# Cycle steps first: a new order of work in seven slots of a two-layer kernel's first attention phase

## Chip, cores and metric

The kernel runs on one core of a Trainium2 chip. The metric is the device time of one execution in microseconds (us). Engines are named as in the profile: PE (TensorE matmul), PEld (its weight loads), DVE (VectorE), ACT (ScalarE), POOL (GpSimd), SP (SyncE, here a DMA queue).

## The reference, cut to what matters

Two layers work on x of 32 sequences, 128 positions, 128 channels, in fp32. Each layer adds an attention block and a feed-forward block to x. Only the first layer is touched by the change:

```
h   = modulated(x, cond_1024)                 # per-sequence scaling around a 128x128 weight
x   = x + causal_attention(h, 16 heads of 64, length 256) @ W_out
f,i = sigmoid(x @ W_f.T + b_f), sigmoid(x @ W_i.T + b_i);  c = x @ W_h.T + b_h
F   = gated recurrence over the positions with f/(f+i+eps) and i/(f+i+eps)*c, starting from cond_1024
g   = sigmoid of a three-layer gelu net on the mean of F over positions
for cycle in 0, 1, 2:
    t = sigmoid of a four-layer gelu net on F (widths 128, 64, 32, 1)
    F = F + (0.1 + range*(0.7*g + 0.3*t - 0.5)*2) * twist(F)      # twist: channel quarters exchanged, with signs
x   = x + F
```

The second layer begins with a mixture of four experts of which two are chosen per sequence from means of x (`routed` computes the choice), then attention with 16 heads of 8, a low-rank modulated layer, and a slot-attention block. Its code is unchanged but for the moment at which the choice of experts and some constants are computed.

## The kernel before

x is held transposed in SBUF as 8 column groups of 128 x 512 (`col(g)`, 4 sequences of 128 positions each).

**The first phase** is a loop over h = 0..15 (a group g = h//2 and one half of the heads) and b = 0..3 (a sequence). One pass of the inner loop is called a *slot* here and numbered 4h+b, so 0 to 63. `unit(h, b)` returns the stages of one attention unit:

- `scores`: 16 matmuls and 2 mask matmuls into two PSUM banks; per bank a DVE maximum (tile `s_max`, 128x384 in), a minimum and an addition (`s_sb<-ps,s_max`); then on ACT four 128x128 exponentials and one 128x256; then POOL folds the rows (`s_half`, two `s_part`), DVE sums and inverts (`s_sum`), and POOL multiplies (`s_sb<-s_sb,s_sum`).
- `turned`: six transposes on PE; the four large ones are copied to `pT` by ACT (128x512), the two small ones by DVE (128x256).
- `values`: 16 small matmuls, copied to `oT` by DVE.
- `projected`: only for b = 3; four matmuls, added to `col(g)` by DVE.

`Staggered(0, 3, 4, 5)` runs, in each slot, the scores of the newest unit, `turned` of the unit three slots older, `values` of the one four older and `projected` of the one five older, in this order. Each slot also issues three of the twelve 128x512 projection matmuls (*pieces*) of h+1; their results go through ACT (`qk`, `v`), and for v an SP transfer (`vo`).

Woven between are generators, one step per slot: `recurrence(g)` starts at b = 1 of each odd h from 3 on (3 matmuls, ACT sigmoids, then on DVE two reciprocals of 128x256, eight scans and one scan of 128x512, with POOL products between). `twisted(g0, cyc, turned)` is one cycle for two groups; it runs at b = 2 of h = 6, 7, 8 (groups 0 and 1, cyc 0, 1, 2: slots 26, 30, 34), of h = 10, 11, 12 (slots 42, 46, 50) and of h = 14 (slot 58, cyc 0). Later cycles run in the second phase. It has four stages: `first` (cn_w1, two gelus of 128x512), `second` (cn_w2), `third` (cn_w3), `fourth` (cn_w4, two tanhs, then the coupling: on DVE `th` from a scalar_tensor_tensor; with cyc 0 a twist matmul whose bank is TF, otherwise TF is the tile `tw`; v = th x F on POOL; th x TF on DVE; F + th; tw = TF - v). In a slot with a cycle the stages alternate with the pieces: first, piece, second, piece, third, piece, fourth, all after the attention stages of that slot. In slot 58 `prepared()` (constants of the second layer) is issued before `first`. `routed` starts at b = 3 of h = 8 and 12 (slots 35 and 51), one step per slot.

**Order.** A scheduler may reorder PE, DVE and POOL instructions; ACT calls made through `act` keep program order, and instructions issued while `pinned` is set keep theirs (DVE and PE). The exponential and the gelu need different ACT tables, and a change between them shows as ACT_TABLE_LOAD.

**PSUM** has 8 banks, given out in turn by `ps()` (ring `AABBBCCC`), so a matmul into a bank waits for the reader of the bank's earlier content.

Nearly all calls go through helpers, so the profile gives line 259 for PE, DVE and POOL and line 383 for ACT; tiles, not lines, tell the operations apart.

Of the kernel before, what the change touches and what calls it, by code (L numbers as in the profile page):

```python
# [11 lines left out]
F32 = mybir.dt.float32  # L12
# [3 lines left out]
AF = mybir.ActivationFunctionType  # L16
ALU = mybir.AluOpType
AX = mybir.AxisListType

P = 128  # L20
# [5 lines left out]
CH = CB * S  # L26
# [192 lines left out]
class Staggered:  # L219
# [7 lines left out]
        self.items.append(stages)  # L227
        self._step()

    def _step(self):  # L230
        for k, lag in enumerate(self.lags):
            n = self.t - lag
            if 0 <= n < len(self.items) and k < len(self.items[n]) and self.items[n][k]:
                self.items[n][k]()
        self.t += 1

    def flush(self):
# [7 lines left out]
def program(ctx, tc, out, xT, packs, where):  # L245
    nc = tc.nc
    pinned = []
# [17 lines left out]
    V, T, G, A = Pinned(nc.vector, pinned), Pinned(nc.tensor, pinned), Pinned(nc.gpsimd, pinned_g), nc.scalar  # L265
# [17 lines left out]
    def w(name):  # L283
        pack, rows, c0, n = where[name]
        return loaded[pack][:rows, c0 : c0 + n]
# [6 lines left out]
    short = []  # L292

    def bank(tag):
        return psum.tile([P, 512], F32, tag="ps" + tag, name="ps", bufs=RING.count(tag))

    def ps():
        if short:
            return bank("C")
        turn["all"] += 1  # L300
        return bank(RING[(turn["all"] - 1) % 8])
# [5 lines left out]
    def mm(out_, lhsT, rhs, start=True, stop=True):  # L307
        T.matmul(out_, lhsT=lhsT, rhs=rhs, start=start, stop=stop)
# [9 lines left out]
    def tt(eng, out_, a, b, op):  # L318
        eng.tensor_tensor(out_, a, b, op)
# [10 lines left out]
    def b3(ap):  # L330

        return ap.rearrange("p (b s) -> p b s", s=S)
# [48 lines left out]
    def act(*args, **kwargs):  # L381

        return tc.keep_in_program_order(A.activation(*args, **kwargs))  # L383
# [7 lines left out]
    tpool = ctx.enter_context(tc.tile_pool(name="t2", bufs=2, side="right"))  # L391
# [29 lines left out]
    ar3 = const("ar3", w("arange"), 0.3)  # L421

    hTs, qks, vs, oTs = {}, {}, {}, {}

    def modulated(g):
        bs = slice(g * CB, (g + 1) * CB)
# [34 lines left out]
    def unit(h, b):  # L461
# [4 lines left out]
        g = h // 2  # L466
        cs = bass.ts(b, S)
        q2 = slice(b * S, b * S + 64), slice(b * S + 64, b * S + S)
        at = {}
# [49 lines left out]
        def turned():  # L519
            pT = apool.tile([P, 6, S], F32, tag="pT", name="pT", bufs=3)  # L520
            p = ps()
            for i in range(4):
                T.transpose(p[:, bass.ts(i, S)], at["s"][:, i, :], ident)
            act(pT[:, 0:4], b3(p), AF.Copy)
            p = ps()
            for i in range(2):
                T.transpose(p[:, bass.ts(i, S)], at["s"][:, 4 + i, :], ident)
            V.tensor_copy(pT[:, 4:6], b3(p)[:, 0:2])
            at["pT"] = pT
# [24 lines left out]
    Fs = {}  # L554
# [39 lines left out]
    def twisted(g0, cyc, turned):  # L594

        gs = (g0, g0 + 1)
        bs = slice(g0 * CB, (g0 + 2) * CB)
        nb = 2 * CB
        at = {}

        def first():
            at["h1"] = []
            for g in gs:
                p = ps()
                mm(p, w("cn_w1"), Fs[g])
                h1 = mpool.tile([P, CH], F32, tag="h1", name="h1")
                act(h1, p, AF.Gelu, bias=w("cn_b1"))
                at["h1"].append(h1)
            if cyc == 0:
                gct = mpool.tile([P, nb], F32, tag="gct", name="gct")  # L610
                for k, g in enumerate(gs):
                    V.tensor_reduce(gct[:, k * CB : (k + 1) * CB], b3(Fs[g]), AX.X, ALU.add)
                V.tensor_scalar(gct, gct, 1.0 / S, None, ALU.mult)
                p = ps()
                mm(p[:64, :nb], w("gc_w1"), gct)
                at["g1"] = mpool.tile([64, nb], F32, tag="g1", name="g1")
                act(at["g1"], p[:64, :nb], AF.Gelu, bias=w("gc_b1"))

        def second():

            p = ps()
            for k in range(2):
                mm(p[64 * k : 64 * k + 64], w("cn_w2"), at["h1"][k])
            at["h2"] = mpool.tile([P, CH], F32, tag="h2", name="h2", bufs=1)
            act(at["h2"], p, AF.Gelu, bias=w("cn_b2"))
            if cyc == 0:
                p = ps()
                mm(p[:32, :nb], w("gc_w2"), at["g1"])
                at["g2"] = mpool.tile([32, nb], F32, tag="g2", name="g2")
                act(at["g2"], p[:32, :nb], AF.Gelu, bias=w("gc_b2"))  # L630

        def third():
            p = ps()
            for k in range(2):
                r = slice(64 * k, 64 * k + 64)
                mm(p[32 * k : 32 * k + 32], w("cn_w3")[r], at["h2"][r])
            at["h3"] = mpool.tile([64, CH], F32, tag="h3", name="h3", bufs=1)
            act(at["h3"], p[:64], AF.Gelu, bias=w("cn_b3"))
            if cyc == 0:

                p = ps()
                mm(p[:, :nb], w("gc_w3"), at["g2"])
                tg = mpool.tile([P, nb], F32, tag="tg", name="tg")
                act(tg, p[:, :nb], AF.Tanh, bias=hb3, scale=0.5)
                cBs[g0] = mpool.tile([P, nb], F32, tag="cB", name="cB")
                V.tensor_scalar(cBs[g0], tg, ar7, 0.1, ALU.mult, ALU.add)

        def fourth():
            two = [ps(), ps()]
            for k in range(2):  # L650
                r = slice(32 * k, 32 * k + 32)
                mm(two[k], w("cn_w4")[r], at["h3"][r])
            for k, g in enumerate(gs):
                th = mpool.tile([P, CH], F32, tag="th", name="th")
                act(th, two[k], AF.Tanh, bias=hb4, scale=0.5)
                cB = cBs[g0][:, k * CB : (k + 1) * CB]
                V.scalar_tensor_tensor(b3(th), b3(th), ar3, inner(cB, S), ALU.mult, ALU.add)

                F, TF = Fs[g], turned[k]
                if cyc == 0:  # L660
                    p = ps()
                    mm(p, w("twist"), F)
                    TF = p
                if cyc < 2:
                    v = mpool.tile([P, CH], F32, tag="h1", name="v")
                    tt(G, v, th, F, ALU.mult)
                tt(V, th, th, TF, ALU.mult)
                tt(G if k else V, F, F, th, ALU.add)
                if cyc < 2:
                    tt(V if cyc == 0 else G, turned[k], TF, v, ALU.subtract)  # L670
                if cyc == 2:
                    tt(G, col(g), col(g), Fs[g], ALU.add)

        return [first, second, third, fourth]


    picks = {}
# [2 lines left out]
    def routed(g0):  # L680
# [3 lines left out]
        def rt(shape, name, dt=F32):  # L684
            return mpool.tile(shape, dt, tag="r_" + name, name="r_" + name, bufs=1)

        seg = rt([P, 3, nb], "seg")
        x3 = X[:, g0 * CH : (g0 + 2) * CH].rearrange("p (b s) -> p b s", s=S)
        for k, (s0, s1) in enumerate(((0, LH), (LH, 2 * LH), (2 * LH, S))):
# [8 lines left out]
        p = ps()  # L698
# [47 lines left out]
        p = ps()  # L746
# [74 lines left out]
    NH = 2 * NCH  # L821
# [3 lines left out]
    pipe = Staggered(0, 3, 4, 5)  # L825
    turned = {}
    running = []
    for h in range(NH):


        pieces = projections(h + 1) if h + 1 < NH else []
        for b in range(CB):
            pipe.push(*unit(h, b))
            for gen in list(running):
                if next(gen, gen) is gen:
                    running.remove(gen)
            if b == 1 and h >= 3 and h % 2 == 1:
                gen = recurrence((h - 3) // 2, [apool.tile([P, CH], F32, tag="rec%d" % i, name="rec", bufs=1) for i in range(3)])
                next(gen)
                running.append(gen)  # L840
            if b == 0 and h % 2 == 0 and h + 2 < NH:
                modulated(h // 2 + 1)
            work = []
            k = h - 6
            if h == NH - 1 and b == 2:
                pinned_g.append(True)
            if b == 2 and 0 <= k < NH - 7 and k % 4 < 3:
                if k % 4 == 0:
                    turned = [tpool.tile([P, CH], F32, tag="t2", name="tw") for _ in range(2)]
                work = twisted(2 * (k // 4), k % 4, turned)  # L850
                if h == NH - 2:
                    prepared()
            if b == 3 and k >= 0 and k % 4 == 2:
                running.append(routed(2 * (k // 4)))
            for i in range(4):
                if work:
                    work[i]()
                if i < 3 and pieces:
                    pieces[3 * b + i]()

# [662 lines left out]
    for i in range(END + 2 * TURN):  # L1525
        r, k = i // TURN, i % TURN
# [6 lines left out]
        if r < NP and k == 0:  # L1533
            ins, outs, _ = (p + q for p, q in zip(experts(2 * r), experts(2 * r + 1)))
# [3 lines left out]
        if k >= 24 and r < NP:  # L1538
            b = k - 23
# [49 lines left out]
```

## Time and profile before

| | |
|---|---|
| median of 3 runs | 1241.89 us (1239.4 to 1242.4) |
| profiled execution | 1240.1 us, span 1238.3 us |
| PE busy | 1083.7 us, 88% of the span |
| DVE busy | 752.8 us, 61% |
| ACT busy | 695.8 us, 56% |
| POOL busy | 447.9 us, 36% |
| mean granted TensorE clock | 0.954 |

Busy time is the union of an engine's instructions; an idle PE shows where a chain through other engines ends late. In the waits view a line tells which engine waited, for whom, how long in total, how often, and the longest. In a timeline a line has the start and duration, the engine, the operation with output and inputs by tile name, and in brackets the idle time before it with what ended it. In the windows view the columns are the window, its length, busy time and count of PE, PEld, DVE, ACT and POOL, then the granted clock, the DMA share and GB/s.

### The profile page before, as it was taken

The page shows a single profiled execution, that of the slowest core. Times are in us where ns is not written, and L with a number is a line of the kernel's source. Part 1 is how long each engine was busy: PE and PEld are TensorE (multiplying, and loading weights), DVE is VectorE, ACT ScalarE, POOL GpSimd, SP SyncE. Part 2 cuts the span into 40 slices and gives each one's busy share as a digit, 9 for nine tenths or more (in the row PEclk, how much of TensorE's full clock was granted, in tenths as well). Part 3 has the DMA queues.
Part 4 walks back from the last instruction along what each step waited for, and adds up shares of the span by engine and source line. Part 5 has one row for each costly group of instructions (what it writes and reads, how often), then busy time and mean ns, then how long its engine had stood idle before and what let it go on. Part 6 is the DMA issues. An engine that isn't in the chain of part 4 may idle for free. (4 is left out here: it accounts for less than half of the span.)

```text
span 1238.3 us, 28744 instructions
## 1 busy us (share of the span) xinstructions
PE 1083.7 (88%) x11429; PEld 694.1 (56%) x11429; DVE 752.8 (61%) x2253; ACT 695.8 (56%) x1668; POOL 447.9 (36%) x557
## 2 busy tenths in 40 slices
PE   3999999988999889898978667998999899998774
PEld 1556565444554445555544345776676677676543
DVE  1455858474784756847355388466756684667554
ACT  1655455555545555436355466666865587558631
POOL 1454545445454454523354531133213321222000
PEclk9999999999999899989989898999999999999867
DMA  6000000000000000000332300233023402320000
GB/s 269 19 10 11 10 10 10 10 4 7 10 11 10 3 8 10 10 3 8 116 115 66 103 23 3 78 109 132 12 78 109 148 12 76 96 67 11 2 17 17
DMA packets 23460, 56.46 MB, mean 46 GB/s; under 512 B 2592, under 2 KB 12960, under 8 KB 23072
## 3 DMA queue, kind: packets, MB, share of 16 engines
q0 software_dynamic: 9648, 40.01, 10.4%
q1 hardware_dynamic: 13104, 13.58, 3.8%
q8 instruction: 90, 1.47, 0.5%
q10 hardware_dynamic: 576, 1.05, 0.2%
q14 instruction: 42, 0.34, 0.1%
HBM read 46.25 MB, written 2.10 MB: 39 GB/s over the span
## 5 line engine op out<-in xcount | busy, mean ns | idle before, releaser
L383 ACT ACTIVATE s_sb<-ps,s_max 128x128 f32<-128x128 f32 x256 | 74.1, 367 | 123.1 <-DVE s_sb L259 119.9
L259 PE MATMUL ps<-hT,w_attn 128*128 128x512 f32 x256 | 125.7, 618 | 15.9 <-DVE hT L259 11.1
L259 POOL TENSOR_TENSOR s_sb<-s_sb,s_sum 128x512 f32<-128x512 f32 (+1 forms) x126 | 106.8, 869 | 67.5 <-DVE s_sum L259 59.8
L383 ACT ACT_TABLE_LOAD x63 | 80.8, 1283 | 79.9 <-DVE s_sb L259 53.6
L259 POOL DMA_INDIRECT ew<-in_expert,rows x64 | 63.6, 995 | 129.1 <-DVE ye L259 79.7
L383 ACT ACTIVATE qk<-ps 128x512 f32<-128x512 f32 x128 | 72.5, 608 | 57.9 <-PE ps L259 57.4
L259 POOL TENSOR_TENSOR s_half<-s_sb 128x256 f32<-128x256 f32 x62 | 46.7, 753 | 126.7 <-ACT s_sb L383 113.2
L259 DVE TENSOR_REDUCE s_max<-ps 128x6 f32<-128x384 f32 x128 | 64.2, 539 | 46.3 <-PE ps L259 46.2
L383 ACT ACTIVATE he<-ps,ew 128x128 f32<-128x128 f32 x256 | 71.8, 386 | 31.7 <-issue 18.4
L259 PEld LDWEIGHTS ps<-qk 64*64 64x64 f32 x2048 | 54.4, 136 | 62.6 <-ACT s_sb L383 22.9
L259 PEld LDWEIGHTS ps<-hT,w_attn 128*128 128x128 f32 x256 | 47.2, 195 | 74.9 <-issue 44.6
L259 PE MATMUL ps<-pT,v 128*64 128x64 f32 (+1 forms) x1536 | 84.0, 229 | 4.8 <-DVE X L259 3.1
L383 ACT ACTIVATE s<-ps,s1max 128x128 f32<-128x128 f32 x256 | 73.3, 391 | 19.0 <-DVE s1max L259 18.9
L259 PEld LDWEIGHTS ps<-pT,v 128*64 128x64 f32 (+1 forms) x1536 | 70.7, 138 | 23.4 <-issue 4.9
L259 PE MATMUL ps<-he,ew 128*128 128x128 f32 x512 | 76.4, 290 | 5.4 <-ACT he L383 4.5
L259 PEld LDWEIGHTS ps<-he,ew 128*128 128x128 f32 x512 | 67.2, 195 | 24.3 <-ACT he L383 13.3
L259 PE MATMUL ps<-qk 64*64 64x128 f32 (+1 forms) x2048 | 65.2, 255 | 15.8 <-ACT s_sb L383 13.4
L259 PE MATMUL ps<-X,ew 128*128 128x128 f32 x512 | 76.6, 281 | 0.2 <-DMA ew<-in_expert,rows 0.2
L259 DVE TENSOR_REDUCE s_sum<-s_part 128x8 f32<-128x256 f32 x62 | 25.8, 416 | 83.3 <-POOL s_part L259 83.3
L259 DVE TENSOR_REDUCE s1m<-ps 128x6 f32<-128x384 f32 x128 | 64.9, 547 | 16.6 <-PE ps L259 16.6
L259 PEld LDWEIGHTS ps<-X,ew 128*128 128x128 f32 x512 | 66.7, 192 | 10.8 <-issue 9.2
L259 PE MATMUL ps<-w_base,s 128*128 128x128 f32 x384 | 61.9, 287 | 7.9 <-ACT s L383 4.8
(302 smaller groups left out, 2539.1 us busy)
## 6 DMA issues: line engine op xcount, KB each, us to landing
vo<-v SPq DMA_DIRECT2D x64, 64.0 KB, 1.9
v1o<-v SPq DMA_DIRECT2D x8, 256.0 KB, 3.6
out_x<-ot SPq DMA_DIRECT2D x8, 256.0 KB, 2.3
X<-in_xT ACTq DMA_DIRECT2D x4, 256.0 KB, 7.3
X<-in_xT SPq DMA_DIRECT2D x4, 256.0 KB, 9.3
w_attn<-in_attn POOLq DMA_DIRECT2D x1, 1024.0 KB, 9.0
w_lowr<-in_lowr SPq DMA_DIRECT2D x1, 1024.0 KB, 12.5
ew<-in_expert,rows POOLq DMA_INDIRECT x64, 5.2
```

The source lines that it names most:

```text
L259: ins = f(*args, **kwargs)
L383: return tc.keep_in_program_order(A.activation(*args, **kwargs))
```

## The change

Seven slots (26, 30, 34, 42, 46, 50, 58) get another order, and two smaller things move.

1. In a slot with a cycle, `first` is issued before everything else; then `turned`, with both of its copies on DVE; then the generators' steps; a piece; `values` and `projected`; `second`; a piece; `third`; a piece; `fourth`. The slot's own scores come last, followed by `coupled`, a new fifth stage of the cycle that holds the coupling; both are pinned. `fourth` keeps cn_w4 and the tanhs and, with cyc 0, issues the twist matmuls into two banks that are kept until `coupled` reads them.
2. v = th x F runs on DVE, except in the second phase (`short`), where it stays on POOL.
3. `routed` yields twice before it starts (not in the second phase).
4. `prepared()` in slot 58 comes after the cycle instead of before it.

```diff
@@ class Staggered
+    def comes(self, *stages):
+        self.items.append(stages)
+
+    def stages(self, *ks):
+        self._stages(ks)
+
+    def newest(self):
+        self._stages(range(1))
+        self.t += 1
+
+    def _stages(self, ks):
+        for k in ks:
+            n = self.t - self.lags[k]
             if 0 <= n < len(self.items) and k < len(self.items[n]) and self.items[n][k]:
                 self.items[n][k]()
+
+    def _step(self):
+        self._stages(range(len(self.lags)))
         self.t += 1
@@ turned
-            act(pT[:, 0:4], b3(p), AF.Copy)
+            if on_vector:
+                V.tensor_copy(pT[:, 0:4], b3(p))
+            else:
+                act(pT[:, 0:4], b3(p), AF.Copy)
@@ twisted
+            at["th"] = []
             for k, g in enumerate(gs):
                 th = mpool.tile([P, CH], F32, tag="th", name="th")
                 act(th, two[k], AF.Tanh, bias=hb4, scale=0.5)
+                at["th"].append(th)
+            at["TF"] = turned
+            if cyc == 0:
+                at["TF"] = [ps(), ps()]
+                for k, g in enumerate(gs):
+                    mm(at["TF"][k], w("twist"), Fs[g])
+
+        def coupled():
+            for k, g in enumerate(gs):
+                th = at["th"][k]
                 cB = cBs[g0][:, k * CB : (k + 1) * CB]
                 V.scalar_tensor_tensor(b3(th), b3(th), ar3, inner(cB, S), ALU.mult, ALU.add)
 
-                F, TF = Fs[g], turned[k]
-                if cyc == 0:
-                    p = ps()
-                    mm(p, w("twist"), F)
-                    TF = p
+                F, TF = Fs[g], at["TF"][k]
                 if cyc < 2:
                     v = mpool.tile([P, CH], F32, tag="h1", name="v")
-                    tt(G, v, th, F, ALU.mult)
+                    tt(G if short else V, v, th, F, ALU.mult)
                 tt(V, th, th, TF, ALU.mult)
...
-        return [first, second, third, fourth]
+        return [first, second, third, fourth, coupled]
@@ routed
+        if not short:
+            yield
+            yield
         seg = rt([P, 3, nb], "seg")
@@ the loop over h and b
-            pipe.push(*unit(h, b))
+            k = h - 6
+            cycle = b == 2 and 0 <= k < NH - 7 and k % 4 < 3
+            work = []
+            if cycle:
+                if k % 4 == 0:
+                    turned = [tpool.tile([P, CH], F32, tag="t2", name="tw") for _ in range(2)]
+                work = twisted(2 * (k // 4), k % 4, turned)
+                work[0]()
+                pipe.comes(*unit(h, b))
+                on_vector.append(True)
+                pipe.stages(1)
+                on_vector.pop()
+            else:
+                pipe.push(*unit(h, b))
...
-            if b == 2 and 0 <= k < NH - 7 and k % 4 < 3:
-                if k % 4 == 0:
-                    turned = [tpool.tile([P, CH], F32, tag="t2", name="tw") for _ in range(2)]
-                work = twisted(2 * (k // 4), k % 4, turned)
-                if h == NH - 2:
-                    prepared()
             if b == 3 and k >= 0 and k % 4 == 2:
                 running.append(routed(2 * (k // 4)))
-            for i in range(4):
-                if work:
-                    work[i]()
-                if i < 3 and pieces:
-                    pieces[3 * b + i]()
+            for i in range(3):
+                if pieces:
+                    pieces[3 * b + i]()
+                if work:
+                    if i == 0:
+                        pipe.stages(2, 3)
+                    work[i + 1]()
+            if work:
+                pinned.append(True)
+                pipe.newest()
+                work[4]()
+                pinned.pop()
+                if h == NH - 2:
+                    prepared()
```

More of the change, by code (lines that the diff above doesn't have):

```diff
@@ L228, in push @@
         self._step()
-    def _step(self):
-        for k, lag in enumerate(self.lags):
-            n = self.t - lag
+    def comes(self, *stages):
[8 more added lines that the diff above has]
+            n = self.t - self.lags[k]
             if 0 <= n < len(self.items) and k < len(self.items[n]) and self.items[n][k]:
                 self.items[n][k]()
+    def _step(self):
+        self._stages(range(len(self.lags)))
         self.t += 1
@@ L423, in program @@
     hTs, qks, vs, oTs = {}, {}, {}, {}
+    on_vector = []
     def modulated(g):
@@ L842, in program @@
                 modulated(h // 2 + 1)
-            work = []
-            k = h - 6
             if h == NH - 1 and b == 2:
                 pinned_g.append(True)
-            if b == 2 and 0 <= k < NH - 7 and k % 4 < 3:
-                if k % 4 == 0:
-                    turned = [tpool.tile([P, CH], F32, tag="t2", name="tw") for _ in range(2)]
-                work = twisted(2 * (k // 4), k % 4, turned)
+            if b == 3 and k >= 0 and k % 4 == 2:
+                running.append(routed(2 * (k // 4)))
+            for i in range(3):
[10 more added lines that the diff above has]
+                pinned.pop()
                 if h == NH - 2:
                     prepared()
-            if b == 3 and k >= 0 and k % 4 == 2:
-                running.append(routed(2 * (k // 4)))
-            for i in range(4):
-                if work:
-                    work[i]()
-                if i < 3 and pieces:
-                    pieces[3 * b + i]()
     right.close()
```

## The prediction

> **What bounds the kernel now.** I read the page first, then PE's waits, then a table of windows over the slots that carry a cycle, then two timelines.
>
> ```profile
> span 1238.3 us, 28744 instructions
> PE 1083.7 (88%) x11429; PEld 694.1 (56%) x11429; DVE 752.8 (61%) x2253; ACT 695.8 (56%) x1668; POOL 447.9 (36%) x557
> ```
>
> PE is busy 88% of the span and no other engine passes 61%, so time is lost where PE stops. The diff only moves work between 205 and 567 us. The waits of PE between 34 and 576 us (what it waited for, total us, times, longest):
>
> ```profile
> PE ps L259 <- ACT s_sb L383: 18.8, 14, 4.1
> PE ps L259 <- ACT h L383: 10.4, 6, 3.9
> PE ps L259 <- DVE pT L259: 5.2, 7, 1.3
> ```
>
> The waits end on ACT's exponentials (s_sb), on the cycles' gelus (h) and on the small copy of the transposes (pT). The windows view gives, for the slots 26–28 (cycle step cyc 0), 30–32 (cyc 1), 34–36 (cyc 2), then 46–48 (cyc 1 of the next pair), the busy time of PE, PEld, DVE, ACT, POOL, then the granted clock:
>
> ```profile
> 213.20:247.00 33.80, 31.69 (x271) 16.84 (x270) 16.14 (x41) 18.37 (x40) 16.00 (x22) 0.95 0.04 9
> 255.40:293.80 38.40, 30.32 (x265) 16.11 (x264) 28.66 (x52) 18.64 (x37) 21.55 (x24) 0.91 0.04 9
> 299.60:328.60 29.00, 27.09 (x259) 14.43 (x258) 16.40 (x45) 17.32 (x35) 14.86 (x20) 1.00 0.04 10
> 410.00:450.00 40.00, 31.95 (x264) 16.48 (x264) 28.76 (x52) 18.66 (x37) 20.53 (x23) 0.87 0.03 8
> ```
>
> PE stands still 8.1 us in each cyc 1 stretch and about 2 in the others, and the clock is below 1. Windows placed on the dips show the clock's own price:
>
> ```profile
> 237.60:241.00 3.40, 3.40 (x39) 2.83 (x37) 2.84 (x9) 1.87 (x6) 2.10 (x4) 0.51 0.25 61
> 418.60:425.40 6.80, 5.58 (x10) 1.27 (x10) 5.42 (x11) 3.51 (x6) 3.41 (x4) 0.50 0.00 1
> ```
>
> A dip lasts 3.4 us or twice that at half clock with PE busy, so it costs about 1.7 us per 3.4 us. It follows a stretch in which PE stood still; the dip at 237.6 came after gaps of only 0.66 and 0.92 us (at 234.00 and 235.07).
>
> The timeline of the first stall in slot 30 (start, duration, engine; in brackets idle before and its releaser):
>
> ```profile
> 259.92 1.28 ACT L383 ACT_TABLE_LOAD   x1 [3.81 <-DVE s_sb L259]
> 262.53 0.61 ACT L383 ACTIVATE pT<-ps 128x512 f32<-128x512 f32 x1
> 263.16 1.28 ACT L383 ACT_TABLE_LOAD   x1
> 264.46 1.27 ACT L383 ACTIVATE h<-ps,w_base 128x512 f32<-128x512 f32 x2
> 265.20 1.97 PE L259 MATMUL ps<-h,w_mix 128*64 128x512 f32 x3 [3.95 <-ACT h L383]
> ```
>
> DVE was held by the recurrence's reciprocals, so the slot's exponentials came late; ACT keeps its order, so the first gelus stood behind exponentials, copy and table load, and cn_w2 waited for them. The second stall, in slot 31:
>
> ```profile
> 273.80 2.99 POOL L259 TENSOR_TENSOR v<-th,F 128x512 f32<-128x512 f32 x2 [4.15 <-DVE th L259]
> 277.73 1.50 DVE L259 TENSOR_TENSOR F<-F,th 128x512 f32<-128x512 f32 x1
> 279.15 0.68 DVE L259 TENSOR_TENSOR th<-th,tw 128x512 f32<-128x512 f32 x1
> 280.18 1.28 ACT L383 ACT_TABLE_LOAD   x1 [6.66 <-DVE s_sb L259]
> 282.15 1.13 PE L259 MATMUL ps<-qk 64*64 64x128 f32 x16 [4.13 <-ACT s_sb L383]
> ```
>
> Recurrence and coupling together kept DVE from s_max; a DVE operation of 128x512 takes 1.50 us while POOL works and 0.68 after it.
>
> **The change, part by part.** A 0.3% step (3.7 us) is about what a measurement of this kernel can tell from no change. The sum is made against the profiled execution, 1240.1 us, which is 1.8 below the median of 1241.89.
>
> *First step ahead, both copies on DVE, scores last (cyc 1, slots 30 and 46).* The gelus of first no longer queue behind exponentials: the 3.95 and 3.94 us go. One table load (1.28 us) goes too: sigmoid to gelu directly. The pT copy of ACT, 0.61 us, becomes a DVE copy of 0.68 (row oT<-ps). What is late next: scores(30) is now the slot's last work, and piece 2 of slot 31 writes the bank that its exponentials free. In the changed order DVE takes s_max(30) after the whole recurrence, which ended at 271.6 before; two score groups of 0.97 us moved behind it and one copy of 0.68 moved ahead, so it starts near 270.3. Reduce, minimum and two exponentials (0.54+0.15+0.28+2x0.28) free the bank at about 271.9; PE is there at 270.2 once the first stall is gone: 1.7 us of idle. The second stall, 4.13 and 4.10, becomes the wait in slot 32 for s_max(32), interleaved with the coupling: between 0 (DVE clear) and 3.3 (two th-type products stretched by 0.8 each and two s_max groups in front); I take 1.7, the middle, as the rows lie on both sides. Old cost: 8.1 idle + 3.4 of clock (dips at 265.0 and 282.0) = 11.5; second time 8.0 + 5.1 (dips of 6.8 and 3.4 us) = 13.1. New cost: 1.7 + 1.7 + half a dip 0.9 = 4.3, from 1.7 to 6.7. Gains: 7.2 (4.8 to 9.8) and 8.8 (6.4 to 11.4).
>
> *v on DVE.* Ten products leave POOL (v group, mean 1.51 us) for DVE at 0.68. In slots 30–32 DVE then holds 28.66 + 0.68 + 2x0.68 = 30.7 us against PE's 30.3: the gain of 7.2 (38.4 to 31.2) just fits, and a larger one needs the stretched products to shrink.
> If v is stretched as the row of 277.73 is (1.50 against 0.68), the four v of the two cyc 1 stretches cost 4 x 0.82 = 3.3 us of a bound DVE, from 0 where POOL is idle; I take 0, since POOL's own ten v (15 us) are gone.
> The Trainium skill speaks against this move: "GPSIMD Engine Reference", section Key points, says that POOL shares its SBUF interfaces with VectorE and collides with DVE instructions of two SBUF inputs, which v is; by it all ten would meet POOL's normalising, and the gain would be about 13 instead of the 16 below.
>
> *cyc 2 (slots 34, 50).* The gaps 0.67 (h) and 1.24 or 1.33 (pT) go, as first and copies are early and nothing is held: 1.9 + 2.0 = 3.9 (2 to 3.9, should the small copy stay late).
>
> *cyc 0 (slots 26, 42, 58).* fourth now also issues the two twist matmuls into banks that are held until coupled reads them. DVE reaches tw only after s_max(26), s_max(27), s_sum(26) (which waits for POOL's half, 0.73, and parts, 0.46 + 0.45), th, v. By those rows tw(0) ends at 236.7 to 238.5, and piece 3 of slot 27, which needs the bank, is reached by PE at 234.6: 2.1 to 3.9 us, taken as 3.0. Behind that piece wait all of PE's later scores. With 0.75 for piece 1 (exponentials of 26) and 0.4 elsewhere 4.15, and 1.7 for a dip: 5.85, from 3.3 (no dip) to 7.5. Old cost of 26–28: gaps 0.53 + 0.66 + 0.92 and one dip of 1.7 = 3.8, a loss of 2.0 (gain 0.5 to loss 3.7). Slot 42 had 2.2 and no dip: loss 3.7 (1.1 to 5.3). Slots 58–60 had gaps of 3.2 and dips of 10.2 us (5.1), together 8.3; prepared() now follows the cycle and fills part of the hold, at one more table load of ACT (1.28 us, hidden, as ACT is busy for 16.8 of the 41.6 us there): gain 2.8 (loss 1 to gain 5).
> On the clock the skill and the trace differ: "TensorE: Matmul & The Clock Gate", section on HAM oscillation, asks for gaps of PE above about 3.4 us before the clock falls, while here 0.51 was granted at 237.6 after gaps of 0.66 and 0.92. By the page the new stalls of 3 us would cost no clock, which makes the gain some 7 us larger, about 23; I stay with the row.
>
> *routed two slots later.* Its reduces (0.50 us each) leave slot 35 for 36, its chain of small DVE operations moves to slots 39–41, where PE already waits 1.11 and 0.93 us for DVE (at 359.07 and 363.75). Loss 1.0 for both times together (gain 0.8 to loss 2). The rest (POOL's F additions, SP's vo transfers in the same slots) keeps its order, and the later phase gets the same instructions; where its clock windows fall moves it by up to 3 us either way (two dips).
>
> Sum: 7.2 + 8.8 + 3.9 - 2.0 - 3.7 + 2.8 - 1.0 = 16.0 us. Profiled 1240.1 - 16.0 = 1224.1; against the median 1241.9 - 16.0, about 1226. All low ends together give a gain of 1.2 (4.8 + 6.4 + 2.0 - 3.7 - 5.3 - 1.0 - 2.0), all high ends 30.3 (9.8 + 11.4 + 3.9 + 0.5 - 1.1 + 5.0 + 0.8).
>
> **Rivals.**
> *A smaller gain: DVE is the new bound in cyc 1.* For it: 30.7 us of DVE in a stretch that shall last 31.2, with waits inside it. Then one stall of 4.1 stays in each cyc 1 stretch with its dip instead of the 1.7 + 0.9: 2 x (5.8 - 2.6) = 6.4, plus about 3 for stretched v: gain 7, 1235. Against it: in 9.7 us of the 38.4 DVE had nothing to do.
> *No change: the stall only moves on,* from slot 31 to slot 32 in both cyc 1 stretches (4.1 + 1.7 kept twice, 11.6 less the 5.2 counted: 6.4), and the cyc 0 holds reach their upper ends (1.7 + 1.6 + 3.8 more): 16.0 - 6.4 - 7.1 = 2.5: 1239.
> *Slower: scores last leave the exponentials too little cover.* Between scores of a cycle's slot and the piece that needs their banks lie only scores, transposes, values and one piece, about 4 us of PE (1.06 + 0.75 + 1.3 + 0.9); s_max, exponentials and an ACT table load need 3.5 when DVE is free. The pinned coupling makes that likely to fail: its first th waits for the tanh, and the next slots' s_max stand behind it on DVE, ACT's exponentials and PE's next piece behind those. If DVE is late by 3 to 4 us in all seven cycles, each pays 4.1 (as PE's wait for s_sb at 278.02) and a dip 1.7, 40.6 in all, plus 3 x 2.1 for the held banks and 1 for routed: 47.9, against old costs of 11.5 + 13.1 + 3.9 + 3.8 + 2.2 + 8.3 = 42.8: 5 slower, 1247. It decides from about 6 us per cycle on; I count 4.3, 0 and 5.9 for cyc 1, 2 and 0.
> That the moves don't happen is no case: the instruction order of the changed kernel has the gelus first and the scores last.
>
> **Chances.** Forecast 0.61, smaller gain 0.17, no change 0.08, slower 0.14. Faster by over 0.3% is the first two, 0.78. The range takes the forecast's low and high ends short of their extremes and all of the smaller gain: 1212 to 1242; above it lies mostly the slower case, below it some 0.05.
>
> **What would show it.** Right: no wait of PE on h above 1 us, ACT_TABLE_LOAD gone between recurrence and gelus, slots 30–32 at 29 to 34 us; a new wait of PE on DVE tw near slot 27, 43 and 59, of 2 to 4 us, with a dip behind; PE's waits for s_sb shorter. Wrong: slots 30–32 still above 36 us, waits above 2 us in slots 34–36, the tw wait absent or above 5 us, or more half clock in total than the 30.6 us of before in this phase.

## The result and the profile after

The changed kernel is slower by 0.4%: 1244.63 us (median of 9 runs, 1241.39 to 1247.05) against 1240.01 us for the kernel before (9 runs, 1237.11 to 1244.65), ratio 1.0040 with a 95% interval of 1.0026 to 1.0053. The forecast was 16 us faster with a range of 1212 to 1242. The direction was wrong.

The page of the changed kernel's profiled execution (1241.51 us, the second shortest of the nine, so the profile shows less of the loss than the medians do):

```profile
span 1239.7 us, 28728 instructions
PE 1085.3 (88%) x11429; PEld 694.7 (56%) x11429; DVE 763.5 (62%) x2270; ACT 691.8 (56%) x1661; POOL 444.6 (36%) x547
```

DVE has 10.7 us more, ACT and POOL a few less, PE is as busy as it was. The waits of PE between 34 and 576 us:

```profile
PE ps L274 <- ACT s_sb L398: 11.3, 13, 1.5
PE ps L274 <- DVE tw L274: 7.3, 2, 4.6
PE ps L274 <- DVE X L274: 7.2, 3, 3.4
PE ps L274 <- DVE s_sb L274: 4.9, 4, 1.3
PE ps L274 <- DVE r_rank L274: 3.6, 1, 3.6
```

The wait on h (10.4 us in six waits before) is no longer among them and the waits on s_sb have lost their two of 4.1 us. In their place stand three kinds that hardly existed: PE waits for DVE's tw (the held twist banks), for X, and for r_rank, a step of the choice of experts. The waits on DVE's s_sb are new too, 1.15 to 1.30 us each near slots 27, 31, 43 and 47; the forecast had 0.75 and 1.7 us there.

The windows view, for slots 26–28, 30–32, 34–36 and 46–48 of the changed kernel (the same four as shown of before), then slot 41, then the dip in slot 28 (length, busy time of PE, PEld, DVE, ACT, POOL, granted clock):

```profile
214.00:251.50 37.50, 31.48 (x271) 16.18 (x270) 18.83 (x44) 17.83 (x39) 14.67 (x20) 0.91 0.03 8
259.80:290.20 30.40, 27.35 (x261) 13.88 (x259) 26.95 (x52) 15.00 (x32) 16.15 (x16) 1.00 0.04 11
297.00:323.20 26.20, 26.12 (x259) 13.59 (x257) 15.91 (x36) 15.01 (x32) 13.74 (x16) 1.00 0.05 11
416.80:449.20 32.40, 28.51 (x265) 14.03 (x263) 27.59 (x53) 16.73 (x35) 17.88 (x19) 0.97 0.04 10
359.90:372.70 12.80, 8.92 (x79) 5.42 (x79) 9.52 (x36) 3.83 (x10) 5.35 (x9) 0.73 0.00 1
239.00:245.90 6.90, 5.76 (x38) 3.42 (x39) 6.90 (x15) 2.44 (x6) 3.42 (x3) 0.51 0.09 21
```

The two cyc 1 windows are 30.4 and 32.4 us where they were 38.4 and 40.0, at nearly full clock. The cyc 0 window is 37.5 us where it was 33.8, and slot 41, which lasted 7.4, lasts 12.8 us at a clock of 0.73.

Where the time went is read from the start of the first scores matmul of a slot (in a changed slot: of its first matmul) to that of a later slot. The means of three profiles of each kernel, in us:

| stretch (slots) | holds | before | changed | difference | forecast |
|---|---|---|---|---|---|
| 25–29 | cyc 0 | 39.37 | 44.48 | +5.1 | +2.0 |
| 29–33 | cyc 1 | 47.86 | 38.69 | -9.2 | -7.2 |
| 33–37 | cyc 2 | 34.87 | 33.01 | -1.9 | -1.9 |
| 37–41 | first step of the choice | 33.47 | 36.28 | +2.8 | with the next row |
| 41–42 | last steps of the choice | 7.43 | 12.43 | +5.0 | +0.5 |
| 42–45 | cyc 0 | 32.09 | 36.67 | +4.6 | +3.7 |
| 45–49 | cyc 1 | 47.52 | 40.05 | -7.5 | -8.8 |
| 49–53 | cyc 2 | 34.95 | 32.35 | -2.6 | -2.0 |
| 53–57 | first step of the choice | 32.60 | 35.31 | +2.7 | with the next row |
| 57–58 | last steps of the choice | 7.70 | 11.56 | +3.9 | +0.5 |
| 58–61 | cyc 0, prepared() | 40.70 | 40.32 | -0.4 | -2.8 |
| 61–end | second phase | 672.85 | 673.45 | +0.6 | 0 |

The differences sum to +3.2 us, near the 4.6 between the medians. What was forecast to be gained came. The losses are in cyc 0 (+9.3 in all against a forecast of +2.9) and around the choice of experts (+14.4 against +1.0).

The timeline of slots 27 and 28 of the changed kernel (start, duration, engine; in brackets the idle time before and its releaser):

```profile
233.33 0.70 DVE L274 SCALAR_TENSOR_TENSOR th<-th,ar,cB 128x512 f32<-128x512 f32 x1
234.07 1.41 DVE L274 TENSOR_TENSOR v<-th,F 128x512 f32<-128x512 f32 x1
237.49 0.42 DVE L274 TENSOR_REDUCE s_sum<-s_part 128x8 f32<-128x256 f32 x1 [2.01 <-POOL s_part L274]
237.82 0.68 DVE L274 TENSOR_TENSOR th<-th,ps 128x512 f32<-128x512 f32 x1
...
239.14 0.68 DVE L274 TENSOR_TENSOR tw<-ps,v 128x512 f32<-128x512 f32 x1
...
239.88 2.07 PE L274 MATMUL ps<-w_attn,hT 128*128 128x512 f32 x2 [4.61 <-DVE tw L274]
```

v takes 1.41 us while POOL works (a product runs there from 233.49); then DVE stands 2.01 us for slot 27's s_sum, which the scheduler put ahead of th x TF; only then comes tw, and PE has waited 4.61 us for the bank. In slot 41, first in the kernel before (two lines), then in the changed one:

```profile
363.85 0.68 DVE L259 TENSOR_TENSOR X<-X,ps 128x512 f32<-128x512 f32 x1
...
364.68 0.41 PE L259 MATMUL ps<-w_base,s_sb 128*128 128x128 f32 x2 [0.93 <-DVE X L259]
```

```profile
361.91 0.90 DVE L274 TENSOR_TENSOR r_gt<-r_gl 8x16 f32<-8x16 f32 x1
...
363.43 0.96 DVE L274 TENSOR_TENSOR r_gt<-r_gt,r_eq 8x16 f32<-8x16 f32 x1
364.32 0.67 DVE L274 TENSOR_TENSOR X<-X,ps 128x512 f32<-128x512 f32 x1
364.92 0.15 DVE L274 TENSOR_REDUCE r_rank<-r_gt 8x4 f32<-8x16 f32 x1
...
365.14 0.50 PE L274 MATMUL ps<-w_base,s_sb 128*128 128x128 f32 x2 [3.60 <-DVE r_rank L274]
```

Operations of 8x16 elements, two of them nearly a microsecond each, stand ahead of X<-X,ps, whose bank PE needs for its transposes. PE waited 0.93 us for X<-X,ps at this place before and waits 3.60 us now. The profile names r_rank, which ended last; that the bank's reader is X<-X,ps is read from slot 57, where a like wait of 3.36 us is put down to X. And in slot 37, the first line again from the kernel before:

```profile
318.43 1.27 POOL L259 TENSOR_TENSOR X<-X,F 128x512 f32<-128x512 f32 x1
```

```profile
322.48 1.27 POOL L274 TENSOR_TENSOR X<-X,F 128x512 f32<-128x512 f32 x1
323.79 0.91 DVE L274 TENSOR_REDUCE r_seg<-X 128x8 f32<-128x336 f32 x2 [0.56 <-POOL X L274]
...
326.47 0.68 DVE L274 TENSOR_TENSOR X<-X,ps 128x512 f32<-128x512 f32 x1
...
327.21 0.98 PE L274 MATMUL ps<-pT,v 128*64 128x64 f32 x17 [1.94 <-DVE X L274]
```

POOL's second X + F of cyc 2 ended at 319.70 before, 8.9 us ahead of slot 37's scores; now it ends at 323.75, 0.5 us behind them, and the reduces of the choice that need it stand ahead of X<-X,ps.

### The profile page after: what moved, and what is told of

It is laid out like the page before. It is cut to its first block, busy times and chain, and to the rows that moved or that the text cites. A ratio compares the mean times of both kernels' runs of the same rounds, so it can differ in the third digit from the quotient of the medians.

```text
span 1239.7 us, 28728 instructions
## 1 busy us (share of the span) xinstructions
PE 1085.3 (88%) x11429; PEld 694.7 (56%) x11429; DVE 763.5 (62%) x2270; ACT 691.8 (56%) x1661; POOL 444.6 (36%) x547
## 3 DMA queue, kind: packets, MB, share of 16 engines
q0 software_dynamic: 9648, 40.01, 10.4%
## 5 line engine op out<-in xcount | busy, mean ns | idle before, releaser
L274 PE MATMUL ps<-hT,w_attn 128*128 128x512 f32 x256 | 131.0, 636 | 18.8 <-DVE hT L274 11.2
L274 POOL TENSOR_TENSOR s_sb<-s_sb,s_sum 128x512 f32<-128x512 f32 (+1 forms) x126 | 115.3, 937 | 62.4 <-DVE s_sum L274 55.0
L274 PE MATMUL ps<-pT,v 128*64 128x64 f32 (+1 forms) x1536 | 87.8, 233 | 9.7 <-DVE X L274 7.4
L274 PEld LDWEIGHTS ps<-pT,v 128*64 128x64 f32 (+1 forms) x1536 | 73.8, 142 | 34.5 <-DVE X L274 8.9
L274 PE MATMUL ps<-w_attn,hT 128*128 128x512 f32 x128 | 66.7, 637 | 9.6 <-DVE tw L274 4.6
L274 PEld LDWEIGHTS ps<-X,ew 128*128 128x128 f32 x512 | 66.9, 193 | 10.7 <-issue 9.2
```

Of the source, the lines that this page charges most:

```text
L274: ins = f(*args, **kwargs)
```

## The experiments

The ratios are to the kernel before, run on the same chip beside each kernel; a "stretch" is one of the table above, taken from that kernel's one profile against the first profile of before.

**The choice of experts at once** (changed kernel without the delay):

```diff
-        if not short:
-
-            yield
-            yield
         seg = rt([P, 3, nb], "seg")
```

> The changed kernel, but routed starts at once, as before the change. Theory A (the delayed choice of experts costs): in the changed kernel the some twenty small DVE operations of the choice stand in slots 41 and 57 ahead of X<-X,ps and hT, and PE waits there 3.6 and 3.4 us, each with a clock dip behind it; without the delay these waits fall to about the 1.1 and 0.9 (and 1.1 and 1.5) us of before, and the time falls by 5 to 8 us, to some 1237 to 1239.5. Theory B (the cyc 0 slots alone cost): the waits on DVE tw near 235 and 395 us stay and the time stays within 2 us of the changed kernel. Both expect the 1.9 us wait on X in slots 37 and 53 to stay, since the reduces of seg are scheduled at the same place.

Measured: 1246.12 us, ratio 1.0060 (1.0044 to 1.0077): no faster than the changed kernel. Slots 41 and 57 did give back their waits (stretch 41–42 at -0.1 where it was +5.4, 57–58 at +1.6 where it was +2.9). But 42–45 went to +7.5 and 58–61 to +8.2.

```profile
PE ps L274 <- DVE tw L274: 10.1, 2, 5.5
```

The wait on tw near slot 43 grew from 2.7 to 5.45 us. The first tw ends 12.2 us behind that slot's scores, 0.7 us later than in the changed kernel, and PE meets the held bank already at the values of slot 43 (393.58) instead of at the transposes after them (398.03). In the changed kernel the choice's own matmul falls into slot 43 and takes one bank of the ring; that this shift is what moves the wait was not tested. In 58–61 no wait is put down to tw: there are 2.81 and 1.83 us on s_sb, and 27.3 us at half clock where the changed kernel had 6.8 to 10.2. So theory A was right about slots 41 and 57 and wrong about the total. That the held banks took what the delay gave back shows below, where the copies take both losses away.

**v on POOL** (changed kernel):

```diff
-                    tt(G if short else V, v, th, F, ALU.mult)
+                    tt(G, v, th, F, ALU.mult)
```

> The changed kernel, but v = th x F on POOL as before. Theory C (v on DVE helps, since DVE waited for POOL's v): slower than the changed kernel by 2 to 6 us, with the waits of PE on tw in slots 27 and 43 longer by about 1 us (v 1.5 us on POOL behind the normalising of 1.6 us). Rival D (DVE is the bound in the cycle slots): faster by 2 to 6 us, since ten products of 0.7 to 1.4 us leave DVE.

Measured: 1241.23 us, ratio 1.0021 (1.0008 to 1.0035), where the changed kernel had 1.0040: some 2 us faster, at the low end of rival D, though the intervals overlap. Theory C's loss did not come in the total. The stretches show both at work: cyc 1 gained only 4.3 and 5.8 us instead of 8.0 and 7.7 (waits on s_sb of 4.0 us in slots 32 and 48 in place of 1.5), while cyc 0 lost 0.9 and 2.6 instead of 3.6 and 3.7 (the wait on tw 2.8 and 2.4 us). tw itself came no earlier: it ends 12.29 and 11.62 us behind the scores of slots 27 and 43, in the changed kernel 12.23 and 11.55. But while DVE waits for POOL's v (2.83 us in slot 28), the copy oT is already made (234.22), and near slot 27 PE has a piece and two more transposes to run before it meets the held bank.

**cyc 0 in the old order** (changed kernel; the twist matmul back beside its use, prepared() ahead):

```diff
                 work = twisted(2 * (k // 4), k % 4, turned)
+            if cycle and k % 4:
                 work[0]()
                 pipe.comes(*unit(h, b))
...
+            old = work and k % 4 == 0
+            if old:
+                if h == NH - 2:
+                    prepared()
+                work[0]()
```

> The changed kernel, but the three cyc 0 slots (26, 42, 58) keep the old order, with prepared() ahead; cyc 1, cyc 2, v on DVE and the delayed choice as changed. Theory B: the 4.6 and 2.7 us waits on tw and their dips go, and slots 26 to 29 and 42 to 45 give back 3.6 and about 4 us, slot 58 to 61 about 1: 1236 to 1238. Theory A: the large part stays in slots 41 and 57, so no more than 3 us come back (1241.5 or above).

Measured: 1236.61 us, ratio 0.9978 (0.9966 to 0.9990). This is what theory B expected: stretch 25–29 at +0.4, 42–45 at +0.9, and with cyc 0 taken out the change gains. The 3.6 us on r_rank and 3.4 on X in slots 41 and 57 are still there. Slots 58–61 gave nothing back (-0.4, as the changed kernel's mean).

**The twist banks copied out by ACT** (changed kernel):

```diff
         def fourth():
+            if cyc == 0 and not short:
+                for k, g in enumerate(gs):
+                    p = ps()
+                    mm(p, w("twist"), Fs[g])
+                    act(turned[k], p, AF.Copy)
             two = [ps(), ps()]
...
-            if cyc == 0:
+            if cyc == 0 and short:
                 at["TF"] = [ps(), ps()]
```

> The changed kernel, but with cyc 0 the two twist matmuls come ahead of cn_w4 and ACT copies their banks at once into the tiles tw (two ACT copies of 0.61 us more in three slots), so that no bank waits for the coupling. If the held banks are what PE waits for in slots 27 and 43, both waits on tw (4.6 and 2.7 us) fall below 0.5 us and their dips go: 5 to 8 us faster than the changed kernel, about 1237 to 1239.5. If the wait only moves on (to the exponentials, which stand behind the coupling on DVE), waits of 2 us or more on s_sb appear in slots 27, 28, 43 or 44 and less than 2 us is gained.

Measured: 1227.59 us, ratio 0.9906 (0.9891 to 0.9920), some 17 us faster than the changed kernel, twice what was expected. The waits of PE between 205 and 576 us:

```profile
PE ps L274 <- ACT s_sb L398: 8.3, 10, 1.7
PE ps L274 <- DVE X L274: 7.2, 3, 3.4
PE ps L274 <- DVE pT L274: 5.6, 5, 1.3
PE ps L274 <- DVE r_rank L274: 3.6, 1, 3.6
```

Nothing waits for tw, and no wait of 2 us came instead in slots 27, 28, 43 or 44; there is one of 1.68 us on s_sb at the scores of slot 29, and one of 2.38 us in slot 47, where the changed kernel had 1.28. All three cyc 0 stretches are shorter than before the change (25–29 -2.7, 42–45 -1.3, 58–61 -4.2), at two ACT copies of 0.60 us per slot. DVE's coupling ends no earlier (tw at 240.0 us against 239.8); it is only no longer what a bank waits for. That the held banks were the cause of the loss in cyc 0 is shown by this run; the run before it agrees. What is left around the choice stays (41–42 +4.6, 57–58 +3.1).

**The changed kernel a second time** (no edit):

> The changed kernel once more, for a second profile. Theory A (the loss sits in the first phase, by held banks and the delayed choice): the stretches between scores agree with the first profile of it to 1 us each up to slot 57 (slots 25 to 29 +3.6, 41 to 45 +9.1 against before). Rival E (the loss is scatter of the clock in the later phase): the first phase agrees, and the stretch behind slot 61 differs by 2 us or more between the two profiles.

Measured: 1246.29 us. The stretches up to slot 57 agree to 1.5 us with the first profile (25–29 and 42–45 are +5.0 each here), and the part behind slot 61 is 3.9 us longer than in the first profile of before. Both sides were partly right, which was left for three more profiles below.

**Copied out, and the choice at once** (both edits above):

> The twist banks copied out by ACT, and routed at once. In the run with the choice at once alone the 3.6 us wait on the choice left slot 41, but the wait on tw in slot 43 and the waits in slot 58 and 59 grew by more. If held banks are the cause of that growth, it cannot appear here: 4 to 7 us faster than with the copies alone (1227.6), some 1221 to 1224. If the delay of the choice is what gives cyc 0 a free DVE (the rival), the time is 1227 or above.

Measured: 1228.62 us (four runs, two near 1224.5 and two near 1232.7), ratio 0.9900 (0.9856 to 0.9943). 42–45 stays at -1.3 and 58–61 at -0.9, so the waits on tw that grew with the choice at once do not appear, as expected. But the 4 to 7 us expected in the total did not come: it can't be told from that of the copies alone, and lies where the rival had it, whose waits the profile does not show. In the profile slots 41 and 57 gave back 4.7 and 3.2 us, of which 58–61 took 3.3.

**cyc 2's additions on DVE** (on top of the run before it):

```diff
-                tt(G if k else V, F, F, th, ALU.add)
+                tt(G if k and (cyc < 2 or short) else V, F, F, th, ALU.add)
...
-                    tt(G, col(g), col(g), Fs[g], ALU.add)
+                    tt(G if short else V, col(g), col(g), Fs[g], ALU.add)
```

> As the run before it, and in cyc 2 both additions to X and both to F are on DVE (three products of 0.68 us more per cyc 2 slot, none of POOL's 1.3). In the changed kernel DVE waits for POOL's second X + F in front of X<-X,ps, and PE waits 1.9 us for that in slots 37 and 53, with a dip behind. If POOL's late additions are the cause, both waits fall below 0.5 us and another 4 to 7 us are gained against the run before. If the reduces of seg and X<-X,ps are late in any case, the waits stay above 1 us.

Measured: 1228.21 us, ratio 0.9886 (0.9860 to 0.9912): no gain that can be told. The wait on X left slots 37 and 53, and another took its place:

```profile
PE ps L274 <- DVE r_agg L274: 3.4, 2, 1.7
```

PE now waits for the agg of the choice, whose matmul stands in its queue, and 37–41 and 53–57 are no shorter (+3.9 and +3.6, where the run before it had +3.1 and +3.4). POOL's additions alone were not what made it late; that the whole chain of coupling, X and choice was is argued.

**Only the delay** (kernel before, with the two yields):

```diff
+        if not short:
+            yield
+            yield
         seg = rt([P, 3, nb], "seg")
```

> The kernel before with nothing but the two yields ahead of routed: the disputed price of the delay by itself. The prediction had 1 us of loss for both choices; theory A now says about 2.9 us for each choice, 4 to 8 us slower than before (1243 to 1247), with a wait of PE for DVE of 3 us or more in slots 41 and 57. If the delay is harmless in the old order, the time stays within 2 us of before.

Measured: 1248.27 us, ratio 1.0053 (1.0033 to 1.0074), with both waits of the changed kernel and no others new (waits between 205 and 576 us):

```profile
PE ps L259 <- DVE r_rank L259: 3.6, 1, 3.6
PE ps L259 <- DVE X L259: 3.4, 1, 3.4
```

41–42 is +4.6 and 57–58 +4.1, while 37–41 and 53–57 are -0.4 each. The disputed term, by itself, is about 6 us of loss. Slots 37 and 53 lose nothing here, so their loss in the changed kernel is not the delay's.

**Only cyc 1 in the new order** (v on DVE; everything else old):

```diff
                 work = twisted(2 * (k // 4), k % 4, turned)
+            if cycle and k % 4 == 1:
                 work[0]()
```

> Only the two cyc 1 slots (30, 46) in the new order, v on DVE in all cycles; cyc 0, cyc 2, prepared() and the choice of experts as before. If the gain of the change sits in cyc 1 and adds up with the rest, slots 29 to 33 and 45 to 49 give back about 8 and 7.5 us as in the changed kernel and nothing else moves by over 1 us: 14 to 16 us faster than before, ratio about 0.988. If the gain of cyc 1 only exists because the cyc 0 slot ahead of it ran late (a rival), the two stretches give less than 5 us each.

Measured: 1233.74 us, ratio 0.9971 (0.9949 to 0.9994), a gain of 3.7 us where 14 to 16 was expected. The stretches did what they should: 29–33 -8.1, 45–49 -8.6, and all others up to 57 within 1.1. But 57–61 is +3.3 and the part behind slot 61 +5.1 in its profile; with the whole of this, its profile is 6.0 us shorter than the first of before. Behind slot 61 PE spent 99.6 us at half clock against 82.5. The instructions there are the same, a few of them in another order, and start 11 us earlier. That the place of the clock windows took the gain fits; it wasn't tested further. The rival is out: the two stretches give all of their gain with cyc 0 in the old order.

**All parts that paid** (cyc 0 and cyc 1 new with the banks copied out, cyc 2 old, the choice at once):

> The parts that paid, together: cyc 0 and cyc 1 in the new order with the twist banks copied out by ACT, cyc 2 in the old order, the choice of experts at once, v on DVE. Adding the stretches of the earlier profiles: -2.7 and -1.3 and -1 to -4 in cyc 0, -6.4 and -7.0 in cyc 1, 0 in cyc 2 and in slots 37 and 53: 18 to 21 us faster than before, ratio 0.983 to 0.986. If the 1.9 us wait on X in slots 37 and 53 stays although cyc 2 is in the old order, cyc 2 is not its cause and the ratio is 0.989 or above.

Measured: 1224.61 us (6 runs), ratio 0.9898 (0.9877 to 0.9919), 12.9 us faster than the kernel before beside it: less than expected in total, though the stretches came as added up (25–29 -2.7, 29–33 -6.3, 42–45 -1.3, 45–49 -7.0, 58–61 -1.0). Slots 37–41 and 53–57 are at +0.0, so with cyc 2 in the old order their loss is gone. The windows of slots 26–28, 30–32 and 34–36:

```profile
213.40:244.60 31.20, 28.82 (x269) 14.92 (x267) 18.50 (x41) 17.19 (x38) 11.70 (x15) 1.00 0.04 9
255.20:285.00 29.80, 27.36 (x261) 13.90 (x259) 26.00 (x52) 14.74 (x31) 16.10 (x16) 1.00 0.04 11
291.90:321.00 29.10, 27.19 (x263) 14.50 (x262) 17.00 (x46) 17.67 (x36) 15.26 (x21) 1.00 0.04 10
```

It beats both kernels; it can't be told from the changed kernel with only the banks copied out (0.9906).

**As that, with the pT copies on ACT:**

```diff
-                on_vector.append(True)
                 pipe.stages(1)
-                on_vector.pop()
```

> As the run before it, but both pT copies keep their old engines (ACT for the large one) in the slots with a cycle. If the copy on DVE matters because ACT holds the gelus there, values and the cycle's steps come later: 1 to 4 us slower than the run before, with new waits of PE on ACT pT in slots 26, 30, 42, 46. If it does not, within 1.5 us of it.

Measured: 1227.82 us, ratio 0.9923 (0.9902 to 0.9943): 3.2 us slower, inside the expectation, though the intervals overlap. The waits are not those expected: none on ACT pT in the cycle slots, but 2.97 us on s_sb in slot 47 (2.37 with the copies on DVE), a gelu late by 1.1 in the cyc 2 slot, and 1.60 on s_sb in slot 31 (0.72). Most of its profile's loss is elsewhere: 58–61 is at +3.1 where it was -1.0, with 20.5 us at half clock against 10.2. So what the place of the copies is worth stays open.

**As that, with v on POOL:**

> As the run with all parts, but v on POOL. In the changed kernel v on POOL cost 1.9 to 3.7 us in each cyc 1 stretch (a wait of 4.0 us on s_sb in slots 32 and 48 in place of 1.5) and gave about as much back where PE waited for tw. With the twist banks copied out nothing waits for tw, so only the cost is left: 4 to 7 us slower than the run with all parts. If v on DVE is worth nothing, within 2 us of it.

Measured: 1236.39 us, ratio 0.9989 (0.9968 to 1.0010), 11.8 us slower than with v on DVE and far beyond the expectation. The waits of PE between 205 and 576 us and DVE in slot 32:

```profile
PE ps L274 <- ACT s_sb L398: 18.8, 10, 4.0
```

```profile
279.37 1.51 DVE L274 TENSOR_TENSOR th<-th,tw 128x512 f32<-128x512 f32 x1 [2.16 <-POOL v L274]
```

DVE waits 2.16 us for POOL's v before it can go on, and s_max and the exponentials wait behind it: 4.0 us of PE in slots 32 and 48 and, unforeseen, 2.8 in slots 28 and 44. Without held banks, v on DVE is worth nearly all of the gain.

**Three more profiles** (no edits), before twice and the changed kernel once:

> A second profile of the kernel before. If the later phase only scatters (clock windows), its length behind slot 61 differs by 2 us or more between profiles of the same kernel, while the stretches up to slot 61 agree to 1 us. If the change lengthened the later phase, all profiles of before agree there to 1 us and those of the changed kernel are longer.

> A third profile of the kernel before, for the same question: scatter of 2 us or more behind slot 61 if clock windows alone set it, agreement to 1 us if the change lengthened the later phase.

> A third profile of the changed kernel: the stretches up to slot 61 within 1.5 us of the first two each; behind slot 61 between +0.8 and +3.9 us against the first profile of before if both were draws of the same scatter.

Measured: 1241.93 and 1239.95 us, and 1243.94 us. Behind slot 61 the three profiles of before have 671.5, 675.3 and 671.7 us, the three of the changed kernel 672.3, 675.4 and 672.7: the same scatter. So the change did not lengthen the second phase; the loss is in the first, where the means differ by 2.6 us. Up to slot 61 the two kernels repeat well except where dips fall (29–33 of before: 46.8 to 49.0, with 6.8 to 13.7 us at half clock).

## Why the prediction was wrong

**What held.** Cyc 1: -9.2 and -7.5 against -7.2 and -8.8, with the new waits about as reckoned (1.3 us for the scores' bank in slot 31, reckoned 1.7; 1.5 in slot 32, reckoned 1.7). Cyc 2: -1.9 and -2.6 against -1.9 and -2.0. The reading of the two 4 us stalls, their causes and what would be late next, was right. DVE did not become the bound, and scores last did not leave the exponentials too little cover: the waits on s_sb went from 18.8 us to 11.3 on ACT's and 4.9 on DVE's. One of the signs did not come: near slot 59 PE waits for no tw. One sign of being wrong did: between 205 us and slot 61 the three profiles of the changed kernel have 34.1, 41.0 and 41.0 us at half clock, those of before 30.7, 23.9 and 30.7. None of the rivals is what happened; the total lies near the one on the slower side for another reason.

**The step "routed two slots later: loss 1.0" failed most.** It priced the moved operations at nothing much because PE already waited there. By itself the delay costs about 6 us (ratio 1.0053), and 8.9 us stand in slots 41 and 57 of the changed kernel. In the new order only the stretches show this price: with the choice at once neither total is lower by more than noise (1.0060 against 1.0040, 0.9900 against 0.9906). The prediction put both waits of before down to DVE; the view gives the 1.11 us to ACT's s_sb and only the 0.93 us to X<-X,ps, and that one is the wait that grew to 3.60. The prediction did not ask what stands behind the choice on DVE. It also counted the some twenty operations as small, where the view of before had r_gt at 0.935 us and r_hot at 0.691 us each. A dip of 6.8 us (slot 41) came on top.

**"Nothing is held" failed for cyc 2.** The stretches of cyc 2 gained what was forecast, but the slots behind them lost it again, and POOL's F additions, of which the prediction said only that they keep their order, were put at nothing. The coupling of cyc 2 ends later when the scores come first, X with it, and the choice's reduces stand ahead of X<-X,ps in the next slot: 2.8 and 2.7 us. Only-delay and all-parts together show it: neither the delay without cyc 2 nor the old cyc 2 without the delay has this loss, and the choice at once with the new cyc 2 has (37–41 +3.0).

**cyc 0 had the right mechanism and too small a size.** The hold was taken as 3.0 us out of 2.1 to 3.9, and was 4.6; near slot 43 it was 2.7, inside. The bound missed the stretched v (1.41, where 0.68 was taken although the row of 277.73 stood beside it) and the 2.01 us for s_sum of slot 27. The clock took 6.8 to 10.2 us at half speed in 25–29, not one window. Slot 58 should have given back 2.8 and gave 0.4: PE's waits in 58–61 fell from 3.2 to 1.4 or 1.5 us, but 6.8 to 10.2 us stayed at half clock.

**Clock and POOL.** Half clock of 3.4 to 6.8 us followed the 2.73 us wait near slot 43 in all three profiles of the changed kernel. The Trainium skill, "TensorE: Matmul & The Clock Gate", section on HAM oscillation, asks for gaps above about 3.4 us, so the row was the better guide. v took 1.41 and 1.18 us beside POOL and 0.68 alone. That agrees with the Trainium skill, "GPSIMD Engine Reference", section Key points, which has POOL contend with DVE instructions of two SBUF inputs. What the prediction drew from that page, a gain smaller by 3 us with v on DVE, fits the changed kernel, where v on POOL was some 2 us faster with overlapping intervals. With the banks freed it is the other way: v on POOL is slower by 11.8 us, since the chain waits for POOL's v.

**Still open:** why kernels whose single profiles are 11 to 17 us shorter up to slot 61 end 4 to 14 us shorter in the median, and why 61–end varies by 4 us in unchanged code. It may go with the time at half clock, whose windows no run here placed on purpose.

## What to carry to other kernels

A bank is held from its first write to its last reader, so a matmul that is issued early for a reader at the end of a long, pinned chain takes a bank from everyone in between; copies by an engine with room (two of 0.60 us in each of three slots) were worth 17 us here. When a step is moved, list what stands behind it in its new place on its queue and which buffers those release, and price small operations by their rows, not by their size. An edit that costs by itself (the delay) and one that is starved (held banks) can hide each other, so undo them together as well as alone, and read the stretches beside the totals.

## What was unexpected of the hardware

DVE operations on 8x16 elements took 0.90 and 0.96 us in slot 41 while POOL's products ran (from 361.74 and 363.33), and another of the same size between them 0.15: beside POOL a tiny operation can cost as much as a 128x512 one. The rows tell how much: the one of 0.96 us ended at 364.39, POOL's product at 364.36. The large ones follow the same pattern. In the changed kernel's profile, up to 580 us, 19 DVE products and sums of 128x512 with both operands in SBUF started while a POOL product ran; each ended 0.55 us behind the end of that product (0.545 to 0.551), after 0.92 to 1.41 us. The 15 that took one operand from a PSUM bank were not stretched (0.67 to 0.69 us). So what v costs beside POOL is what is left of POOL's running product, and 0.55 us. The second phase of the same program took 671.5 to 675.3 us from profile to profile, with 79.1 to 92.7 us of it at half clock.
